# Four small reorderings at the end of a two-layer cross-attention kernel

What is changed: the second MLP weights of the next-to-last batch are built on GpSimd, the delays before three norms of the last batch and after the first turned rows are longer, and in the last layer two kinds of tiles get a second buffer.

## The chip, the cores and the metric

The kernel runs on one core of a Trainium2 chip. The time is the device time of one execution in microseconds (us). The core has five engines, each with its own instruction queue worked off in order: TensorE (PE, matrix products), VectorE (DVE), ScalarE (ACT), GpSimd (POOL) and SyncE (SP, which here only starts DMAs). A transfer that a kernel calls indirect takes its row numbers from a tile and is issued on POOL.

## The reference, cut to what matters

Everything is float32. `x` and the context are 16 batches of 256 rows of 256 numbers. There are two layers, each an attention and an MLP with a residual, with a layer norm before each.

```python
x = x + _L0_xattn_ref(ctx, _layernorm(x), ...)   # 8 heads of 128; keys: context and latents (512)
x = x + _L0_ffn_ref(_layernorm(x), ...)          # 256 -> 1024 -> 256
x = x + _L1_xattn_ref(_layernorm(x), ctx, ctx, ...)
x = x + _L1_ffn_ref(_layernorm(x), ...)          # 8 experts, 256 -> 256 -> 256, gated
```

In the first MLP the weights depend on the batch: products of rows of its own input are added to them.

```python
m1 = (even[:, :4, :, None] * odd[:, :4, None, :]).reshape(Bx, Hx, Dx)
m2 = (even[:, 4:, :, None] * odd[:, 4:, None, :]).reshape(Bx, Dx, Hx)
h = jnp.einsum('bsd,hd->bsh', x, W1) + scale * jnp.einsum('bsd,bhd->bsh', x, m1) + b1
h = jax.nn.gelu(h, approximate=False)
out = jnp.einsum('bsh,oh->bso', h, W2) + scale * jnp.einsum('bsh,boh->bso', h, m2) + b2
```

In the last layer each row has a weight for each of 8 experts, from a sigmoid; weights outside a zone are zero, so a row needs only some of the experts. The output of a row is the weighted sum of its experts, added to the row.

## The kernel before, in words

**Layer 0, attention.** A loop over `n`, the 128 pairs of batch and head, is the backbone. For each pair it computes queries (`s0q`) and keys (`s0k`), scores and softmax (`s1`, scaled on POOL in `s1_scale`, L902), turns the probabilities through DRAM (`s2` transposes blocks of 32 on DVE and sends them, L910 to L914; `s2_fetch` brings them back, L923), and multiplies with the values (`s3`, the product `po`).

**The chain of a batch.** What follows for a batch, output projection (`px`), norm, first MLP (`ph`, gelu, `pf`), norm, second attention (`pv1`, `pq1`, `sc1`, `po1`), norm and routing logits (`pl`), is a Python generator, `chain` (L332). It starts two heads into the next batch. For batches up to 13 (`hopped`) tensors are turned through DRAM; for batches 14 and 15 PE turns them with an identity matrix (`turned_tile`). Each norm sums on DVE, takes the root on POOL (`ln_rstd`, L261 and L262) and is applied on DVE (`ln_apply`, L267). `plus_row` (L312) adds a bias row on POOL.

In the first MLP `w2_block` (L432) multiplies, for each of 4 blocks and 2 halves, rows of the batch with its columns (L435), and `w2_add` adds the fixed weights on DVE (L443). `pf` needs these `W2e` and the gelu's `hT`, which ACT computes after loading a table.

**Routing.** `route` (L628) computes the expert weights of a batch, numbers its rows within each expert (`pn`), and scatters each row into its slot with 16 indirect DMAs per batch on POOL (L718, two at a time between other work).

**The last layer.** `experts` (L1229) runs over groups of up to 4 tiles of 128 rows of one expert. Batches 0 to 9 are the first part (experts 0 to 7, three groups each), batches 10 to 15 the second. A group's rows are loaded from their slots (L1137), turned (the first two groups by PE, `turn_rows`; the others through DRAM, `send_rows` and `fetch_rows`), and go through `gate` (`pg`), `up` (`pu`) and `down` (`pd`). `down` scales the result on DVE into a tile `o` (L1219) and adds it to the output rows in DRAM with an indirect DMA on POOL (L1220), 128 in all. Scatters of one expert have distinct rows and do not wait for each other; the first one of the next expert of the same part waits until those of the expert before have landed.

**What sets the order.** All of it is issued by one program, so each engine's order is the order in which Python calls are made. `Clock.pe` counts the PE time issued so far. A generator yields the PE time to wait before it goes on; `gap` (L114) runs, between the pieces of the backbone and after it, the first job in `line` whose time has come. So the numbers in `yield` decide where a step stands in every engine's queue. The generators of the change are those of batches 13 to 15 and of the experts, which run side by side from the last heads of batch 15 on.

**Pools.** `D_.wk` (L1110) is opened after the last head's scores, `D_.more` (L1113) when the last projection has been issued. A tile asked of a pool with all its buffers in use makes its writer wait.

Of the kernel before, what the change touches and what calls it, by code (L numbers as in the profile page):

```python
# [12 lines left out]
F32 = mybir.dt.float32  # L13
# [6 lines left out]
P = 128  # L20
# [9 lines left out]
def xattn_ffn_kernel(  # L30
# [10 lines left out]
    nc = tc.nc  # L41
    B, S, D = x.shape
# [21 lines left out]
    wk = ctx.enter_context(tc.tile_pool(name="work_c", bufs=1))  # L64
# [3 lines left out]
    def mm_tile(n, name):  # L68
        return psum.tile([P, n], F32, tag="mm", bufs=6, name=name, padded_shape=[P, 512])
# [9 lines left out]
    def mm(out, lhsT, rhs, **kw):  # L79
        nc.tensor.matmul(out, lhsT, rhs, **kw)  # L80
        Clock.pe += max(0.38, 1.667e-3 * math.prod(out.shape[1:]))
# [23 lines left out]
    def apart(ins, group, others=()):  # L105

        for g in (group, *others):
            tc.declare_no_dep(
                ins.ins, group=g, reason="rows of one group go to different places"
            )  # L110
        tc.add_to_no_dep_group(group, ins.ins)
        nc.gpsimd.nop()
# [65 lines left out]
    for k, n in enumerate(NTOKS):  # L178
        t = sum(NTOKS[:k]) // P
# [78 lines left out]
    def ln_rstd(mv, tag):  # L258

        rs = small.tile([P, TC], F32, tag=f"rs{tag}", bufs=2, name=f"rs_{tag}")  # L260
        nc.gpsimd.tensor_scalar(rs, mv[:, :, 1], EPS, None, ALU.add)  # L261
        nc.gpsimd.tensor_tensor(rs, rs, mhalf, ALU.pow)  # L262
        return rs
# [21 lines left out]
    def to_blocks(pool, src, C, tag, bufs, name, most=None):  # L285
        tb = pool.tile(
            [P, C * D], F32, tag=tag, bufs=bufs, name=name, padded_shape=[P, most or C * D]
        )
        tb = tb.rearrange("p (m d c s) -> p m d c s", m=QP, d=DC, c=C)
        for c in range(C):  # L290
            nc.vector.transpose(
                tb.rearrange("p m d c s -> p d m c s")[:, :, :, c, :],
                src[:, c, 0:D].rearrange("p (d m r) -> p d m r", d=DC, m=QP),
            )
        hop = dram.tile([P, QP, DC * C * QB], F32, tag=f"{tag}{C}", name=f"hop_{name}")
        nc.sync.dma_start(hop, tb.rearrange("p m d c s -> p m (d c s)"))
        return hop
# [34 lines left out]
    def chain(b, A, behind):  # L332
# [11 lines left out]

        hopped = b < B - 2

        def raw_tile(tag, name):
            return wk.tile([P, QP, DC, TC, QB], F32, tag=tag, name=name)

# [20 lines left out]


        rs = ln_rstd(mv, "b")
        yield 2.5


        while behind is not None and b - 1 not in A.fed:
# [55 lines left out]
        def w2_block(c):  # L432
            for d in range(DC):

                (nc.gpsimd if hopped else nc.vector).tensor_tensor(  # L435
                    W2e[:, c, d, :].rearrange("p (i a) -> p i a", i=NI),
                    evs[1][:, :, c * NA : (c + 1) * NA],
                    od[:, d, NI : 2 * NI].unsqueeze(2).to_broadcast([P, NI, NA]),
                    ALU.mult,
                )  # L440
# [40 lines left out]
        for c in range(NI):  # L481
            w2_block(c)
            yield 1.7
            w2_add(c)
# [17 lines left out]


        rs = ln_rstd(mv, "q")
        yield 2.5
        while behind is not None and not behind.done:
            yield 0.4
        y = wk.tile([P, TC, D], F32, tag="y", name=f"yc_{b}")
# [7 lines left out]
        sent = Clock.pe + SENT  # L516
# [72 lines left out]

        rs = ln_rstd(mv, "d")  # L590
        nc.sync.dma_start(out[b].rearrange("(c p) d -> p c d", p=P), x_b)

        yield 2.8 if b < B - 1 else 6.0
        while b >= 2 and not A.tails[b - 2].done:
            yield 0.4
        row = A.row[b] = wk.tile([P, TC, ROW], F32, tag="row", bufs=2, name=f"row_{b}")
# [141 lines left out]
    with ExitStack() as sh, ExitStack() as sa, ExitStack() as sf:  # L738
# [352 lines left out]
        def add_chain(b, behind):  # L1091
            job = Job(chain(b, A, behind))
            A.tails[b] = Job(route(b, A, job))
            line.extend([job, A.tails[b]])
            return job


        TG = 4
        NG = TG * P

        class D_:


            w, wk, more = {}, None, None


        def open_front():
# [8 lines left out]
        def load_expert(e):  # L1116
            k = len(D_.w)
            pool = D_.front if k == 0 else D_.wk if k == 1 else D_.more
            w = D_.w[e] = pool.tile([P, 3, DC, D], F32, bufs=1, name=f"wx_{e}")
            nc.sync.dma_start(w[:, 0], Wg[e].rearrange("(c p) i -> p c i", p=P))  # L1120
            nc.sync.dma_start(w[:, 1], Wu[e].rearrange("(c p) i -> p c i", p=P))
            nc.sync.dma_start(w[:, 2], Wd[e].rearrange("(c p) d -> p c d", p=P))

        class G:
# [44 lines left out]
                )  # L1169

            def send_rows(self):
                self.hop = to_blocks(D_.wk, self.rows, self.tiles, "tbd", 1, f"rows_{self.name}_b", TG * D)

            def fetch_rows(self):
                self.take()
# [32 lines left out]
            def down(self, t):  # L1208
                if t >= self.tiles:
                    return  # L1210
                w = D_.w[self.e]
                pd = mm_tile(D, f"pd_{self.name}_{t}")
                for i in range(IC):
                    mm(
                        pd, self.hT[:, i, ts(t, P)], w[:, 2, i, :],
                        start=(i == 0), stop=(i == IC - 1),
                    )
                o = D_.wk.tile([P, D], F32, tag="o", bufs=9, name=f"o_{self.name}_{t}")
                nc.vector.tensor_scalar(o, pd, self.wt[:, t : t + 1], None, ALU.mult)  # L1219
                ins = nc.gpsimd.indirect_dma_start(  # L1220
                    out=out_rows[0 : sum(NTOKS[: self.part + 1]), :],
                    out_offset=bass.IndirectOffsetOnAxis(ap=self.at[:, t : t + 1], axis=0),
                    in_=o, in_offset=None, compute_op=ALU.add,
                )
                apart(
                    ins, f"out_{self.part}_{self.e}", [f"out_{1 - self.part}_{e}" for e in range(E)]
                )

        def experts(groups, ready=None):  # L1229

            if groups[0].e not in D_.w:
                load_expert(groups[0].e)
            for g in groups[:2]:
                g.load()
            yield 7.0
            while D_.wk is None:
                yield 0.4
            for d in range(DC):
                groups[0].turn_rows(d)
                yield 2.0  # L1240
            late = None
            for n, g in enumerate(groups):
                if n == 0:
                    groups[2].load()
                if n + 3 < len(groups):
                    while ready is not None and not ready(groups[n + 3]):
                        yield 0.4
                for i in range(IC):
                    g.gate(i)
                    yield  # L1250
                    g.up(i)
                    yield
                    if n == 0:
                        groups[1].turn_rows(i)
                    if n + 2 < len(groups):
                        if i == 0:
                            groups[n + 2].send_rows()
                        else:
                            groups[n + 2].fetch_rows()
                    if i == 0 and n + 3 < len(groups):  # L1260
                        groups[n + 3].load()
                    if late is not None:
                        late.down(2 * i)
                        late.down(2 * i + 1)
                        yield
                ahead = groups[min(n + 3, len(groups) - 1)].e
                if ahead not in D_.w and (len(D_.w) < 2 or D_.more is not None):
                    load_expert(ahead)
                if n + 2 < len(groups) and groups[n + 2].e not in D_.w:
                    while D_.more is None:  # L1270
                        yield 0.4
                    load_expert(groups[n + 2].e)
                late = g
            for t in range(late.tiles):
                late.down(t)
# [21 lines left out]
        for n in range(NS + 2):  # L1297
            b, h = divmod(n, H)
            if h == 2 and b > 0:
                last = add_chain(b - 1, last)  # L1300
            more = bulk(b, h) if n < NS else None
            if n < NS:
                s1(n)
            if n == NS - 4:
                sf.close()
                open_front()
                rest = Job(experts(
                    lists,
                    lambda g: g.part == 0 or B - 1 in A.tails and A.tails[B - 1].done,
                ))  # L1310
                line.append(rest)
# [48 lines left out]
        with tc.If(some > 0):  # L1360
            drain(experts(groups(0, "+", (4, 3, 3)) + groups(1, "+", (3, 3))))
# [38 lines left out]
```

## Time and profile before

| | |
|---|---|
| median of 3 runs | 1845.97 us (1845.02 to 1847.69) |
| profiled execution | 1845.63 us |
| its span, first to last instruction | 1843.6 us |
| mean granted TensorE clock | 0.994 |
| matmul time on PE | 1808.7 us |
| POOL: scatters to the output, L1220 | 128 of 1.57 us |
| POOL: scatters to the slots, L718 | 256 of 0.99 us |
| last matmul starts at | 1828.05 us |
| last scatter starts at | 1832.96 us |

Times in the profile count from the span's start. A row of the timeline has start, duration, engine, line, operation, output and inputs, and in brackets the idle time before it with what the profile takes for its end. The duration of an indirect DMA on POOL is that of its issue; its data land later. An idle time's releaser is the semaphore event that came last, which need not be the one that was waited for.

### The profile page before, as it was taken

The page shows a single profiled execution, that of the slowest core. Times are in us where ns is not written, and L with a number is a line of the kernel's source. Part 1 is how long each engine was busy: PE and PEld are TensorE (multiplying, and loading weights), DVE is VectorE, ACT ScalarE, POOL GpSimd, SP SyncE. Part 2 cuts the span into 40 slices and gives each one's busy share as a digit, 9 for nine tenths or more (in the row PEclk, how much of TensorE's full clock was granted, in tenths as well). Part 3 has the DMA queues.
Part 4 walks back from the last instruction along what each step waited for, and adds up shares of the span by engine and source line. Part 5 has one row for each costly group of instructions (what it writes and reads, how often), then busy time and mean ns, then how long its engine had stood idle before and what let it go on. Part 6 is the DMA issues. An engine that isn't in the chain of part 4 may idle for free.

```text
span 1843.6 us, 22696 instructions
## 1 busy us (share of the span) xinstructions
PE 1808.7 (98%) x6600; PEld 1230.4 (67%) x6600; DVE 1212.0 (66%) x3349; ACT 583.2 (32%) x1298; POOL 846.4 (46%) x980
## 2 busy tenths in 40 slices
PE   8999999999999999999999999999999999999996
PEld 4666666666666666666667676767676676666664
DVE  5456585858585858586767676757566676655553
ACT  3443333333434333333333333333333321111110
POOL 2123235353535353535353535353524178766655
PEclk9999999999999999999999999999999999999998
DMA  6553546464646465645455556464636478999986
GB/s 223 180 183 121 165 148 203 153 201 153 205 146 205 161 197 161 195 156 198 161 193 164 190 164 197 154 204 146 202 103 222 133 215 193 238 242 225 214 204 100
DMA packets 271181, 332.72 MB, mean 180 GB/s; under 512 B 31388, under 2 KB 222792, under 8 KB 271048
## 3 DMA queue, kind: packets, MB, share of 16 engines
q1 hardware_dynamic: 240280, 279.63, 48.2%
q0 software_dynamic: 30720, 51.54, 12.2%
q8 instruction: 55, 0.90, 0.2%
q14 instruction: 78, 0.64, 0.1%
q10 hardware_dynamic: 48, 0.01, 0.0%
HBM read 165.77 MB, written 165.28 MB: 180 GB/s over the span
## 4 chain that ended last, share of the span: by engine, by line
PE 93%; DVE 3%; DMA 1%; issue 1%; POOL 1%; SPq 0%; ACT 0%; ACTq 0%; DVEq 0%; POOLq 0%
PE po L80 13%; PE pv L80 13%; PE sc L80 13%; PE pk L80 11%; PE pq L80 7%; PE px L80 6%; PE ph L80 6%; PE pg L80 6%; PE pf L80 6%; PE pu L80 5%; PE pd L80 5%; PE pl L80 1%; POOL out_dram L1220 0%; DVE tb L910 0%; PE pn L80 0%
## 5 line engine op out<-in xcount | busy, mean ns | idle before, releaser
L902 POOL TENSOR_SCALAR pr<-pr,ri 128x512 f32<-128x512 f32 x256 | 179.4, 711 | 319.5 <-DVE ri L901 314.5
L894 ACT ACTIVATE pr<-sc,nm 128x512 f32<-128x512 f32 x256 | 173.5, 682 | 478.3 <-DVE nm L888 405.9
L718 POOL DMA_INDIRECT slots_d<-row,at_slot x256 | 253.3, 989 | 70.4 <-issue 70.4
L1220 POOL DMA_INDIRECT out_dram<-o,at x128 | 201.2, 1572 | 100.6 <-issue 26.5
L80 PE MATMUL po<-pT,v 128*128 128x256 f32 x1024 | 242.1, 379 | 1.3 <-DVE W2T L955 0.7
L80 PE MATMUL sc<-kT,qT 128*128 128x512 f32 x512 | 241.1, 593 | 1.5 <-ACT kT L827 1.5
L80 PE MATMUL pk<-kvT,Wk_sb 128*128 128x512 f32 x512 | 240.6, 592 | 0.0
L80 PEld LDWEIGHTS po<-pT,v 128*128 128x128 f32 x1024 | 194.4, 190 | 69.2 <-issue 37.5
L80 PE MATMUL pv<-Wv_sb,kvT 128*128 128x512 f32 x512 | 235.2, 592 | 0.0
L940 DVE TENSOR_SCALAR outT<-po,cvec 128x256 f32<-128x256 f32 x128 | 61.0, 477 | 250.6 <-PE po L80 229.6
L910 DVE STREAM_TRANSPOSE tb<-pr 128x512 f32<-128x512 f32 x256 | 165.8, 685 | 6.9 <-DMA hop<-tb 6.5
L80 PEld LDWEIGHTS pv<-Wv_sb,kvT 128*128 128x128 f32 x512 | 97.1, 190 | 107.3 <-issue 102.1
L888 DVE TENSOR_REDUCE nm<-sc 128x1 f32<-128x512 f32 x256 | 160.2, 662 | 2.0 <-PE sc L80 1.9
L80 PEld LDWEIGHTS sc<-kT,qT 128*128 128x128 f32 x512 | 96.9, 190 | 70.1 <-issue 61.2
L80 PEld LDWEIGHTS pk<-kvT,Wk_sb 128*128 128x128 f32 x512 | 97.3, 190 | 67.8 <-issue 61.2
L80 PE MATMUL pg<-yTd,wx 128*128 128x384 f32 (+3 forms) x328 | 127.1, 510 | 7.9 <-DVE yTd L829 5.7
L80 PE MATMUL pq<-kvT,Wq_sb 128*128 128x256 f32 x512 | 132.8, 382 | 0.0
L1195 ACT ACTIVATE sg<-pg 128x384 f32<-128x384 f32 (+3 forms) x82 | 41.3, 503 | 278.3 <-PE pg L80 244.7
L80 PEld LDWEIGHTS pq<-kvT,Wq_sb 128*128 128x128 f32 x512 | 96.4, 191 | 42.1 <-issue 28.5
L80 PE MATMUL pd<-wx,hTd 128*128 128x256 f32 x512 | 123.9, 379 | 0.6 <-DVE hTd L1206 0.6
L80 PE MATMUL pu<-yTd,wx 128*128 128x384 f32 (+3 forms) x328 | 123.7, 500 | 0.0
L825 ACT COPY v<-pv 128x512 f32<-128x512 f32 (+1 forms) x132 | 70.6, 535 | 164.9 <-PE pv L80 163.9
(205 smaller groups left out, 2700.3 us busy)
## 6 DMA issues: line engine op xcount, KB each, us to landing
hop<-tb SPq DMA_DIRECT2D x128, 512.0 KB
pT<-hop SPq DMA_DIRECT2D x512, 128.0 KB
ev<-ev_d SPq DMA_DIRECT2D x32, 512.0 KB
rows<-slots_d SPq DMA_DIRECT2D x31, 397.5 KB
hop_rows_b<-rows_b SPq DMA_DIRECT2D x30, 384.0 KB
yTd<-hop_rows_b SPq DMA_DIRECT2D x120, 96.0 KB
rows<-slots_d SPq DMA_DIRECT2D x8, 530.0 KB
cin<-in_ctx_dram SPq DMA_DIRECT2D x16, 256.0 KB
```

The lines of the kernel that those rows point to most:

```text
L80: nc.tensor.matmul(out, lhsT, rhs, **kw)
L718: ins = nc.gpsimd.indirect_dma_start(out=slots_d[part], out_offset=bass.IndirectOffsetOnAxis(ap=at_slot[:, c, e : e + 1], axis=0), in_=row ...
L825: nc.scalar.copy(out, src)
L888: nc.vector.tensor_reduce(nm, sc, AX.X, ALU.max, negate=True)
L894: nc.scalar.activation(pr, sc, AF.Exp, bias=nm, accum_out=sm)
L902: nc.gpsimd.tensor_scalar(pr, pr, ri, 1.0, ALU.mult, ALU.mult)
L910: nc.vector.transpose(tb[:, :, c, :], heads[n][c][0].rearrange("p (m f) -> p m f", m=QP))
L940: nc.vector.tensor_scalar(o, po, col("bv", h), None, ALU.add)
L1195: nc.scalar.activation(self.sg, self.pg, AF.Tanh, scale=0.5)
L1220: ins = nc.gpsimd.indirect_dma_start(out=out_rows[0 : sum(NTOKS[: self.part + 1]), :], out_offset=bass.IndirectOffsetOnAxis(ap=self.at[:, ...
```

## The change

1. `w2_block` runs on GpSimd for batch 14 too; only batch 15 keeps it on VectorE.
2. A batch's three delays after a norm's sums are named `queued`: unchanged for batches up to 14 (2.5, 2.5, 2.8), and 6.7, 6.7 and 7.0 for batch 15 (before: 2.5, 2.5, 6.0).
3. After each of the first group's two turns the experts wait 4.0 instead of 2.0.
4. The blocks `tbd` of `send_rows` (one buffer) and the tiles `o` of `down` (nine) are taken in turn from `D_.wk` and, once it is open, `D_.more`, so that there are two and eighteen.

```diff
+        queued = 2.8 if b < B - 1 else 7.0
...
         rs = ln_rstd(mv, "b")
-        yield 2.5
+        yield queued - 0.3
...
-                (nc.gpsimd if hopped else nc.vector).tensor_tensor(
+                (nc.gpsimd if b < B - 1 else nc.vector).tensor_tensor(
...
         rs = ln_rstd(mv, "q")
-        yield 2.5
+        yield queued - 0.3
...
         nc.sync.dma_start(out[b].rearrange("(c p) d -> p c d", p=P), x_b)
-
-        yield 2.8 if b < B - 1 else 6.0
+        yield queued
...
-            w, wk, more = {}, None, None
+            w, wk, more, sent, made = {}, None, None, 0, 0
...
             def send_rows(self):
-                self.hop = to_blocks(D_.wk, self.rows, self.tiles, "tbd", 1, f"rows_{self.name}_b", TG * D)
+
+                D_.sent += 1
+                pool = D_.more if D_.sent % 2 and D_.more is not None else D_.wk
+                self.hop = to_blocks(
+                    pool, self.rows, self.tiles, "tbd", 1, f"rows_{self.name}_b", TG * D
+                )
...
-                o = D_.wk.tile([P, D], F32, tag="o", bufs=9, name=f"o_{self.name}_{t}")
+                D_.made += 1
+                pool = D_.more if D_.made % 2 and D_.more is not None else D_.wk
+                o = pool.tile([P, D], F32, tag="o", bufs=9, name=f"o_{self.name}_{t}")
...
             for d in range(DC):
                 groups[0].turn_rows(d)
-                yield 2.0
+                yield 4.0
```

## The prediction

> **What bounds the kernel now.** I read the page first. It shows TensorE (PE) busy all the way, with GpSimd (POOL) full only in the last stretch.
>
> ```profile
> PE 1808.7 (98%) x6600; PEld 1230.4 (67%) x6600; DVE 1212.0 (66%) x3349; ACT 583.2 (32%) x1298; POOL 846.4 (46%) x980
> PE   8999999999999999999999999999999999999996
> POOL 2123235353535353535353535353524178766655
> PE 93%; DVE 3%; DMA 1%; issue 1%; POOL 1%; SPq 0%; ACT 0%; ACTq 0%; DVEq 0%; POOLq 0%
> ```
>
> The change acts only from about 1420 us on (the last heads of batch 15, and the expert layer). So I asked next what PE waited for after 1395.
>
> ```profile
> PE pg L80 <- DVE yTd L829: 5.7, 1, 5.7
> PE ycT_p L84 <- DVE yc L267: 2.5, 1, 2.5
> PE pg L80 <- DVE o L1219: 1.9, 1, 1.9
> ```
>
> These three holes are what an eye on PE would go for. Third, the timeline of POOL from 1476 to the end, which carries the forecast:
>
> ```profile
> 1478.15 1.10 POOL L718 DMA_INDIRECT slots_d<-row,at_slot  x1 [0.19 <-issue]
> 1479.56 0.97 POOL L718 DMA_INDIRECT slots_d<-row,at_slot  x1 [0.30 <-issue]
> ...
> 1514.51 1.60 POOL L1220 DMA_INDIRECT out_dram<-o,at  x1 [0.30 <-issue]
> 1519.31 1.57 POOL L1220 DMA_INDIRECT out_dram<-o,at  x1 [3.20 <-DMA out_dram<-o,at]
> ...
> 1580.37 1.56 POOL L1220 DMA_INDIRECT out_dram<-o,at  x1 [0.30 <-issue]
> 1587.68 1.55 POOL L1220 DMA_INDIRECT out_dram<-o,at  x1 [5.75 <-DVE sg L1205]
> ...
> 1660.56 1.58 POOL L1220 DMA_INDIRECT out_dram<-o,at  x1 [0.30 <-DMA out_dram<-o,at]
> ...
> 1829.22 1.58 POOL L1220 DMA_INDIRECT out_dram<-o,at  x1 [0.30 <-issue]
> 1831.10 1.55 POOL L1220 DMA_INDIRECT out_dram<-o,at  x1 [0.31 <-DMA out_dram<-o,at]
> 1832.96 1.56 POOL L1220 DMA_INDIRECT out_dram<-o,at  x1 [0.30 <-issue]
> ```
>
> And two rows of VectorE (DVE), the tiles that the scatters of 1660.56 and 1832.96 add into the output:
>
> ```profile
> 1639.24 0.48 DVE L1219 TENSOR_SCALAR o<-pd,wt 128x256 f32<-128x256 f32 x1 [0.38 <-issue]
> 1828.79 0.48 DVE L1219 TENSOR_SCALAR o<-pd,wt 128x256 f32<-128x256 f32 x1 [0.80 <-PE pd L80]
> ```
>
> So POOL is 20.8 us behind at 1660 and still 3.7 us behind at the end. From 1478.15 it stops only where a new expert's first scatter has to wait until the scatters of the expert before have landed (1514.51 to 1519.31, 1580.37 to 1587.68; the releaser named there, an early DVE step, had long been done). The page's chain runs through PE because PE hardly idles; the order of this stage is POOL's. A scatter starts every 1.87 us, a routing scatter (L718) every 1.28, a norm's pair takes 1.25, a row addition (L312) 1.45. With these, 1478.15 plus 16 routing scatters (20.5), a norm (1.25), an addition (1.45) and seven scatters (13.1) gives 1514.45; the row says 1514.51. The queue is full.
>
> **The change, part by part.** The profiled execution took 1845.63 us (span 1843.6, so 2.0 around it), 0.34 under the median of 1845.97; the sum is made against 1845.63. What is moved I take from the instruction order of the two programs.
>
> *Second weights of batch 14 on GpSimd.* Eight blocks (L435) leave DVE (8 x 0.41 = 3.3 us) for POOL (8 x 0.61 = 4.9; median of the 112 such rows of earlier batches). On POOL two stand before the scaling of head 6 (L902), six between that and head 7. POOL is idle there (8.35 us before 1432.75), the rows they read were issued at 1412.19, and head 6's scaling still starts at 1423.0: 0 on the path. The GpSimd rows range only from 0.61 to 1.06 us beside a busy DVE, so I add nothing for interference. The Trainium skill (SBUF — State Buffer, Who interferes with whom) says that a VectorE instruction with two SBUF inputs and a GpSimd instruction that reads SBUF lock each other out; by it the three weight additions on DVE beside the six blocks could each wait 0.61, and the sum below would be 1.8 us longer.
>
> *Turned rows at 4.0 instead of 2.0.* The first gate now stands behind the last MLP's output product (pf, 16 of its 32 passes, then head 5's po, then the rest). PE's first hole does not close, it changes owner: pf needs the gelu. On DVE the blocks' time is partly taken by the norm of batch 13's rows, which now stands ahead of them; the score maxima of head 7 end at about 1429.5 instead of 1430.6. The same ACT rows follow (two exponentials, table load 1.28, gelu 1.91; before, the gelu ended at 1434.74), so pf starts at about 1433.7, against 1432.64 for the gate before. Half clock till 1436.58 as before: PE is 0.5 later.
>
> A second, new wait: the next group's second turned tile is copied by ACT only behind the two exponentials of batch 14's attention. From the end of the scores that took 1.8 us before (1463.5 to 1465.3), plus 0.5 for the copy; the gate there has 0.3 + 0.65 of work to cover it. 1.5 us of hole; between 0 (if ACT gets there first) and 2.4 (the whole of it).
>
> *Where the POOL queue starts.* The first two scatters of expert 0 ran at 1463.20 and 1465.17 in idle time. Now their products come behind the last projection (px) and batch 14's turn, 41.7 us of PE work after pf's start, plus 0.5 and 1.5 as above: about 1476.9. DVE then has the projection's statistics (1.3), the slot numbers (1.2) and four row transposes (1.42) ahead of the tile (0.44): POOL gets it at about 1479.0. Against the old start of 1478.15 that is +0.85; two more scatters in the full queue, +3.74; one norm that now lies before it, -1.25. **+3.4**. Bounds: 1475.4 if nothing on DVE stands before the tile and there is no second hole (-0.2), 1481 with half clock after it (+5.4).
>
> *Which routing scatters lie in a landing wait.* The total of them is the same, the places are not. Before, one pair of batch 14 (1550.82, 1552.10) ran between the last scatter of expert 1 and the first of expert 2, and one of batch 15 in the wait from 1609.63 to 1618.26 (expert 3 to 4). Both cost nothing there. Now each stands behind the wait, among scatters: 2 x 2.56 = **+5.1** (0 to 5.1, 0 if the wait shortens because less is queued ahead). The first wait was 5.62, with tile and landing arriving together; the nearest one without a pair is 4.80 to 5.4: **-0.5**.
>
> *What else is moved past.* On SP the load of the third group's rows goes behind head 7's blocks, from 1435.8 to about 1448; its transposes come at about 1455, and the next such load (issued 1455.77, transposed 1461.12 without a wait) took at most 5.4: hidden. The first load of the second part's rows waits on SP for the last routing scatter, which moves from 1657.4 to about 1669; SP may stand from about 1665 to 1675, with the blocks of two later groups behind it. PE has two groups (some 17 us) in hand by then, so 0; if that cover were gone, PE would stand up to 10 us, of which POOL's backlog swallows all.
>
> *Delays of 6.7, 6.7, 7.0 for batch 15.* They place other PE work before the turn of yc: the second hole (2.46, and half clock 1538.98 to 1542.39, that is 4.2 together) mostly closes. The clock rows are clear: a 3.41 us window with 0.03 us of matmul is followed by one at 0.50. The Trainium skill (TensorE: Matmul & The Clock Gate, Why this matters for your kernels) warns only of gaps over about 3 us; by it this hole would be worth 2.5. Either way it shortens PE alone, worth 0 to 4.2 there and 0 at the end while POOL is behind.
>
> *Two buffers of blocks and 18 output tiles.* They take away the 1.9 us wait for an output tile and waits of the row blocks (0.3 to 0.5 on PE). POOL's scatters use tiles that are ready long before: 0. With cover gone (POOL caught up) all this is worth PE's sum: +0.5 +1.5 -4.2 -0.3 -2.0 -0.5 = -5.0.
>
> Sum: +3.4 +5.1 -0.5 = **+8.0**, so 1853.6 us, 0.4% slower than the median. Of it the thirteen landing waits (4.80 to 8.62, mean 6.3) are taken as they were.
>
> **The rivals.**
> *POOL's queue starts early, or one pair is still hidden.* For it: the lower bounds above. Start at 1475.4 and one pair lost: -0.2 +2.6 -0.5 = +1.9, 1847.5: no difference that a measurement of this kernel tells (0.2%, 3.7 us). Against it: DVE's order before the tile is written in the program.
> *PE is the bound, and all its closed holes count.* POOL must then lose its backlog. One mechanism can do it: PE, with 18 tiles and two block buffers, runs further ahead, its block traffic leaves the DMA queues sooner, and scatters land faster. It decides from a mean landing wait of 5.4 (13 x 0.9 = 11.7 undoes +8.0 and gives -3.7); at the shortest, 4.80, PE limits: -5.0 and the 3.4 us that the last tile waits now, 1837.2. For it: waits without traffic are the short ones. Against it: the traffic's amount is the same, DMA is at 0.9 to 1.0 from 1580 to 1800, and POOL's own pace of 1.87 is untouched.
> *More is lost.* The new hole halves the clock (+1.7), the first one grows by the interference, and the landing waits at the expert changes rise by half a microsecond each because pairs are queued right before them (+6.5): 1858 to 1861.
>
> **How the numbers follow.** Main case (+4 to +12) 0.63; no difference 0.16; PE-bound and faster 0.11; more lost 0.10. Slower by over 0.2%: 0.73. The likeliest is 1853.6, its own range 1849.7 to 1857.6. For 8 in 10 the range takes in the no-difference case and most of the last: 1845 to 1859.5.
>
> **What would show it.** Right: the last scatter on POOL at about 1841 while PE's last matmul ends near 1824; pf waiting for the gelu about 6.7 us near 1427; no long wait of the turn of yc; first output scatter near 1479, and no L718 between the last scatter of expert 1 and the first of expert 2. Wrong: a last scatter within 1 us of the last tile (PE is the bound), landing waits with a mean under 5.4, or the first output scatters before 1476.

## The result, and the profile after

The changed kernel takes 1855.14 us (median of 6 runs, 1854.20 to 1857.64) against 1845.49 us (6 runs of the kernel before): ratio 1.0053, 95% interval 1.0040 to 1.0066. It is slower by 0.5%. The profiled execution took 1854.39 us; its span is 1852.7 us, 9.1 more than before.

The busy times and the 40 slices on the page of the changed kernel, for PE and POOL:

```profile
PE 1810.5 (98%) x6600; PEld 1234.7 (67%) x6600; DVE 1208.8 (65%) x3341; ACT 582.6 (31%) x1298; POOL 852.1 (46%) x988
...
PE   8999999999999999999999999999998999999995
...
POOL 2123235353535353535353535353525177766666
```

PE's matmul time rose by 1.8 us only. An eye on PE would not find nine microseconds here. What PE waited for after 1395 (in total, times, longest), all waits of 0.2 us and more:

```profile
PE pf L80 <- ACT hT L475: 7.1, 1, 7.1
PE pf L80 <- DVE W2e L445: 3.2, 2, 1.9
PE pg L80 <- ACT yTd L826: 0.9, 1, 0.9
PE pd L80 <- DVE hTd L1212: 0.2, 1, 0.2
```

The first hole changed its owner, from the turned rows to the gelu; the waits for `yc` and for an output tile are gone; a wait for the second weights of batch 15 is new, and the prediction did not have it. Third, POOL's timeline (start, duration, instruction, idle time before it), with line numbers eight higher than before for the output scatters (L1228) and one for the routing scatters (L719):

```profile
1480.92 1.68 POOL L1228 DMA_INDIRECT out_dram<-o,at  x1 [2.02 <-DVE o L1227]
...
1545.33 1.59 POOL L1228 DMA_INDIRECT out_dram<-o,at  x1 [0.70 <-DVE o L1227]
...
1555.40 1.60 POOL L1228 DMA_INDIRECT out_dram<-o,at  x1 [0.30 <-issue]
1560.41 1.56 POOL L1228 DMA_INDIRECT out_dram<-o,at  x1 [3.41 <-DVE o L1227]
...
1618.72 1.61 POOL L1228 DMA_INDIRECT out_dram<-o,at  x1 [0.30 <-DVE o L1227]
1624.29 1.56 POOL L1228 DMA_INDIRECT out_dram<-o,at  x1 [3.96 <-DVE o L1227]
...
1841.92 1.56 POOL L1228 DMA_INDIRECT out_dram<-o,at  x1 [0.30 <-issue]
```

The last tile that a scatter adds, on DVE:

```profile
1831.18 0.48 DVE L1227 TENSOR_SCALAR o<-pd,wt 128x256 f32<-128x256 f32 x1 [0.79 <-PE pd L80]
```

The last scatter starts 10.25 us after its tile is finished; before, it was 3.69. POOL sets the end, by more than before. Between the last scatter of expert 1 (1555.40) and the first of expert 2 (1560.41) no routing scatter lies any more, nor between 1618.72 and 1624.29.

**Where the time came from, stretch by stretch.** The execution after runs 0.61 us late already before the change acts (the last transposition of the first turned rows starts at 1427.30, before at 1426.69). So I count both from that transposition. Times to POOL's first scatter of each expert of the first part, of the second part, and to the last scatter; the forecast column adds up the terms of the prediction in the stretches where they fall:

| first scatter of | before | after | difference | forecast |
|---|---|---|---|---|
| expert 2 | 127.85 | 133.11 | +5.3 | +2.9 |
| expert 3 | 160.99 | 169.45 | +8.5 | +5.5 |
| expert 4 | 191.57 | 196.99 | +5.4 | +5.5 |
| expert 5 | 225.65 | 231.28 | +5.6 | +5.5 |
| expert 6 | 251.85 | 259.78 | +7.9 | +8.0 |
| expert 7 | 273.68 | 282.63 | +9.0 | +8.0 |
| second part | 286.71 | 295.68 | +9.0 | +8.0 |
| last scatter | 406.27 | 414.62 | +8.4 | +8.0 |

The end is met within half a microsecond, but two stretches on the way are off, by +2.4 (up to expert 2) and by -3.0 (expert 3 to 4). The experiments below ask whether POOL's queue is the cause at all, which part fills it, and what these two errors are. Times in them are compared by ratio with runs of the kernel before on the same chip; 0.1% is 1.85 us.

### The profile page after: what moved, and what is told of

Its sections match the earlier page's. It is cut to its first block, busy times and chain, and to the rows that moved or that the text cites. A ratio compares the mean times of both kernels' runs of the same rounds, so it can differ in the third digit from the quotient of the medians.

```text
span 1852.7 us, 22641 instructions
## 1 busy us (share of the span) xinstructions
PE 1810.5 (98%) x6600; PEld 1234.7 (67%) x6600; DVE 1208.8 (65%) x3341; ACT 582.6 (31%) x1298; POOL 852.1 (46%) x988
## 5 line engine op out<-in xcount | busy, mean ns | idle before, releaser
L719 POOL DMA_INDIRECT slots_d<-row,at_slot x256 | 253.2, 989 | 70.7 <-issue 69.8
L1228 POOL DMA_INDIRECT out_dram<-o,at x128 | 201.5, 1574 | 96.6 <-DVE o L1227 36.2
L80 PE MATMUL pf<-W2e,hT 128*128 128x256 f32 x512 | 123.6, 391 | 10.4 <-ACT hT L475 7.1
L80 PE MATMUL pq<-kvT,Wq_sb 128*128 128x256 f32 x512 | 133.0, 382 | 0.0
## 6 DMA issues: line engine op xcount, KB each, us to landing
rows<-slots_d SPq DMA_DIRECT2D x31, 397.5 KB
```

The lines of the kernel that those rows point to most:

```text
L719: ins = nc.gpsimd.indirect_dma_start(out=slots_d[part], out_offset=bass.IndirectOffsetOnAxis(ap=at_slot[:, c, e : e + 1], axis=0), in_=row ...
L1228: ins = nc.gpsimd.indirect_dma_start(out=out_rows[0 : sum(NTOKS[: self.part + 1]), :], out_offset=bass.IndirectOffsetOnAxis(ap=self.at[:, ...
```

## Experiments: one part at a time

**The turned rows alone.**

```diff
                 groups[0].turn_rows(d)
-                yield 2.0
+                yield 4.0
```

> The kernel before with the turned rows alone at 4.0. Theory (GpSimd's queue of indirect DMAs sets the end): +6.0 us. The first output scatter comes at about 1479 and takes two more scatters into the full queue (+3.4); in this program's order one pair of routing scatters still lies between the last scatter of expert 1 and the first of expert 2, the other pair has left the change from expert 3 to 4 (+2.6). Rival (TensorE sets the end): its two holes, +0.5 and +1.5, so +2.0 us. A third possibility, that the start alone counts and a pair behind the landing wait costs nothing: +3.4.

Measured: 1858.09 us against 1846.76, ratio 1.0064 (1.0051 to 1.0077), +11.8 us (9.4 to 14.2). This part alone costs the whole loss and more; all three numbers that I had for it were too small. PE's waits in this kernel, the three longest:

```profile
PE pf L80 <- ACT hT L473: 7.9, 1, 7.9
PE pf L80 <- DVE W2e L443: 3.7, 2, 3.0
PE pg L80 <- DVE W1e L427: 1.7, 1, 1.7
```

and POOL's timeline at expert 1:

```profile
1548.11 0.96 POOL L718 DMA_INDIRECT slots_d<-row,at_slot  x1 [0.30 <-issue]
1552.65 1.59 POOL L1220 DMA_INDIRECT out_dram<-o,at  x1 [3.59 <-DVE o L1219]
```

PE stands for the weights of batch 15, the tiles of expert 1 come late, and POOL, which was to be full from 1479 on, runs dry for 3.6 us at 1549. The first scatter of expert 2 comes 137.85 us after the turned rows, 10.0 later than before.

**The delays of batch 15 alone.**

```diff
+        queued = 2.8 if b < B - 1 else 7.0
...
         rs = ln_rstd(mv, "b")
-        yield 2.5
+        yield queued - 0.3
...
         rs = ln_rstd(mv, "q")
-        yield 2.5
+        yield queued - 0.3
...
-        yield 2.8 if b < B - 1 else 6.0
+        yield queued
```

> The kernel before with the delays of batch 15 alone (6.7, 6.7, 7.0). Theory (GpSimd's queue): the queue starts where it did; a pair leaves the wait from expert 3 to 4 (+2.6), a row addition of 1.45 us enters the wait from expert 1 to 2 (-1.45): +1.1 us. Rival (TensorE sets the end): the hole before the turn of yc closes, -4.2 us.

Measured: 1848.01 us, ratio 1.0006 (0.9994 to 1.0017): +1.1 us, between -1.1 and +3.1. The rival's -4.2 is excluded. PE did gain: its last tile comes 397.5 us after the turned rows, before 402.1. POOL's last scatter comes at 408.0, before 406.3. A gain of 4.6 us on the engine that is busy 98% of the span did not reach the end.

**Two buffers alone.**

```diff
-            w, wk, more = {}, None, None
+            w, wk, more, sent, made = {}, None, None, 0, 0
...
-                self.hop = to_blocks(D_.wk, self.rows, self.tiles, "tbd", 1, f"rows_{self.name}_b", TG * D)
+                D_.sent += 1
+                pool = D_.more if D_.sent % 2 and D_.more is not None else D_.wk
+                self.hop = to_blocks(
+                    pool, self.rows, self.tiles, "tbd", 1, f"rows_{self.name}_b", TG * D
+                )
...
+                D_.made += 1
+                pool = D_.more if D_.made % 2 and D_.more is not None else D_.wk
-                o = D_.wk.tile([P, D], F32, tag="o", bufs=9, name=f"o_{self.name}_{t}")
+                o = pool.tile([P, D], F32, tag="o", bufs=9, name=f"o_{self.name}_{t}")
```

> The kernel before with the two block buffers and 18 output tiles alone; the order of GpSimd's instructions is the one of before. Theory (GpSimd's queue): 0.0 us, and TensorE's last product 2.4 us earlier. Rival (TensorE sets the end): -2.4 us.

Measured: 1846.28 us, ratio 1.0001 (0.9990 to 1.0011), +0.2 us between -1.8 and +2.0. The -2.4 of the rival lies outside. PE's last tile moved by 0.6 us only (401.5 after the turned rows), not by 2.4, so the second half of my expectation was too large as well.

**Second weights of batch 14 alone on GpSimd.**

```diff
-                (nc.gpsimd if hopped else nc.vector).tensor_tensor(
+                (nc.gpsimd if b < B - 1 else nc.vector).tensor_tensor(
```

> The kernel before with the second weights of batch 14 alone on GpSimd. Theory: 0.0 us, the eight rows lie in GpSimd's idle time before the queue fills. Rival (the two engines hold each other up at SBUF): +1.8 us. GpSimd rows of 0.61 speak for the first, rows of 1.06 for the second.

Measured: 1845.39 us, ratio 0.9992 (0.9983 to 1.0001), -1.5 us between -3.1 and +0.2. The rule on the shared lock (the Trainium skill, SBUF — State Buffer, Who interferes with whom) could have made it +1.8; the time does not show that. The trace shows rows of both engines slower side by side in one place: the weight addition of 1426.02 on DVE in the changed kernel took 1.07 us, the other three 0.66 to 0.70, and of the eight GpSimd rows the two from 1426.50 on took 1.06 us, the others 0.60 to 0.64. That is the rule's kind of overlap, worth 1.3 us in sum over the two engines, and it did not reach the end. In the profiled execution of this part alone PE's last tile even came 3.7 us earlier than before, its first hole being 4.3 us instead of 5.7.

**All but the turned rows.** The changed kernel with `yield 2.0` back:

> The changed kernel with the turned rows back at 2.0; the other three parts stay. Theory: GpSimd's queue starts as before, and the three parts alone gave +1.1, 0 and -1.5 within about 2 us each: between -1.5 and +1.5 us. Rival (TensorE sets the end): -6.6 us. If the parts add their harm to each other rather than through the queue's start: +3 or more.

Measured: 1844.50 us against 1846.96, ratio 0.9980 (0.9969 to 0.9991), -3.7 us between -5.7 and -1.7. Slightly better than I allowed, and not the rival's -6.6: PE's last tile comes 398.5 us after the turned rows (before 402.1), the last scatter 403.4 (before 406.3), 4.4 us behind its tile. So the other three parts are worth a little, and the turned rows alone turn the gain into a loss.

## Experiments: is it POOL's queue?

**Ten scatters less.** In both kernels the ten output scatters of expert 1 of the first part are left out (the output lacks their rows):

```diff
                 nc.vector.tensor_scalar(o, pd, self.wt[:, t : t + 1], None, ALU.mult)
+                if self.part == 0 and self.e == 1:
+                    return
                 ins = nc.gpsimd.indirect_dma_start(
```

The kernel before without them:

> The kernel before without the ten output scatters of expert 1 of the first part (the output tiles are still made; their rows are missing from the output). Theory (GpSimd's queue sets the end): the queue loses ten scatters (18.7 us) and one landing wait, far more than its backlog at the end (3.7 us), so TensorE's last product sets the end: -3.4 us. Rival (TensorE sets the end already): 0.

The changed kernel without them:

> The changed kernel without the same ten scatters (the same rows are missing). Theory: GpSimd is 10.25 us behind TensorE at the end of the changed kernel; with the backlog gone the end follows TensorE's last product, 10 us earlier: -0.4 us against the kernel before, and 2.4 to 3 above the kernel before without the same scatters, which is TensorE's own sum for the change (the prediction had -5.0 for it). Rival (the time is lost elsewhere than in GpSimd's queue): +9 as in the changed kernel.

Measured: 1839.63 us, ratio 0.9959 (0.9946 to 0.9972), -7.6 us, for the one; 1852.48 us, ratio 1.0022 (1.0009 to 1.0034), +4.1 us, for the other (its runs spread from 1847.4 to 1855.4, and the profiled one, 1854.8, is among the longest). Both expectations missed, the theory's and the rival's. In neither run does PE set the end: the last scatters still start 4.6 and 10.5 us after their tiles are finished. POOL, idle until expert 2, falls behind again from there; in the profiled execution of the changed kernel its last scatter comes 414.9 us after the turned rows, with the ten scatters 414.6. What the missing scatters did change is PE. Its waits after 1395 in the kernel before without the ten scatters:

```profile
PE pg L80 <- DVE yTd L829: 5.7, 1, 5.7
PE pf L80 <- DVE W2e L443: 0.3, 1, 0.3
PE pd L80 <- DVE hTd L1206: 0.2, 1, 0.2
```

The wait for `yc` (2.5 us before) and the one for an output tile (1.9) are gone without any change to delays or buffers. They were POOL's doing: the norm of `yc` takes its root on POOL, and in the kernel before that root stood behind scatters. Its timeline in the kernel before:

```profile
1533.27 1.60 POOL L1220 DMA_INDIRECT out_dram<-o,at  x1 [0.30 <-issue]
1535.18 0.97 POOL L718 DMA_INDIRECT slots_d<-row,at_slot  x1 [0.30 <-issue]
1536.45 0.96 POOL L718 DMA_INDIRECT slots_d<-row,at_slot  x1 [0.30 <-issue]
1537.43 0.26 POOL L261 TENSOR_SCALAR rs_q<-mv_q 128x2 f32<-128x2 f32 x1
```

With POOL idle there (its root at 1533.17), PE's last tile comes 394.8 us after the turned rows, 7.3 earlier than in the kernel before. In the changed kernel PE's waits stay as they were without the ten scatters (7.1, 3.2, 0.9, 0.2), and its last tile comes at 403.9 with or without them. So PE's own price of the change, with the queue out of its way, is +9.1 us. It adds up: the first hole 7.1 instead of 5.7 (+1.5), half clock behind it 2.8 instead of 2.0 (+0.8), the new gate 0.9, the weights of batch 15 3.2 instead of 0.3 (+2.9) and the half clock behind them 3.0.

**What holds the first scatter of expert 2?** From that scatter to the last one POOL needs 275.1 to 283.8 us in all kernels with unchanged group order here (278.4 before, 281.5 after), so of the 8.4 us that the last scatter loses 5.3 lie ahead of that scatter. Two things could hold it: PE's wait for the weights, or the full queue. The two kernels without the ten scatters show PE's side alone, because POOL is idle there until the tile comes (first the kernel before, then the changed one):

```profile
1550.54 1.61 POOL L1222 DMA_INDIRECT out_dram<-o,at  x1 [7.22 <-DVE o L1219]
1560.93 1.61 POOL L1230 DMA_INDIRECT out_dram<-o,at  x1 [7.28 <-DVE o L1227]
```

That is 123.3 and 132.6 us after the turned rows. In the kernel before, the same scatter comes at 127.85, 4.5 us later, held up by the queue and by the hole that the queue makes in PE's work; in the changed kernel PE alone holds it until half a microsecond before its 133.11. DVE in the changed kernel, from the first of these waits on, has no free time (start, duration, instruction):

```profile
1523.58 0.68 DVE L445 TENSOR_TENSOR W2e<-W2e,W2T 128x512 f32<-128x512 f32 x1
1524.18 0.75 DVE L437 TENSOR_TENSOR W2e<-ev,od 128x256 f32<-128x256 f32 x2
1524.85 1.09 DVE L291 STREAM_TRANSPOSE rows_b<-rows 128x256 f32<-128x256 f32 x3
1525.87 0.84 DVE L1227 TENSOR_SCALAR o<-pd,wt 128x256 f32<-128x256 f32 x2
1526.62 0.69 DVE L445 TENSOR_TENSOR W2e<-W2e,W2T 128x512 f32<-128x512 f32 x1
...
1529.03 0.72 DVE L445 TENSOR_TENSOR W2e<-W2e,W2T 128x512 f32<-128x512 f32 x1
```

The last addition (1529.03) was at 1526.04 in the kernel before, where PE waited 0.3 us for it. I took away the four additions (the weights of batch 15 then lack their common part):

```diff
         def w2_add(c):
+            if b == B - 1:
+                return
```

> The changed kernel without the four additions to the second weights of batch 15 on VectorE (its weights lack their common part, so the rows of batch 15 come out different). Theory (GpSimd's queue sets the end): TensorE's two waits for these weights and the half clock behind them, 6.6 us together, go, and its last product comes that much earlier, but GpSimd waited for tiles there by only 0.3 us twice: -0.6 us against the changed kernel, +9 against the kernel before. Rival (TensorE's lost time is what the change costs): -6.6 against the changed kernel, +3 against the kernel before.

then the first two output scatters (their rows are missing):

```diff
+                if self.part == 0 and self.first + t * P < 2 * P:
+                    return
                 ins = nc.gpsimd.indirect_dma_start(
```

> The changed kernel without its first two output scatters (the first two tiles of expert 0; their rows are missing). Theory: they stand at the head of a queue that never runs empty again, so the end comes two scatters earlier, -3.7 us against the changed kernel, +6 against the kernel before. Rival (the queue waits for tiles later, so that its start does not count): 0 against the changed kernel, +9.6 against the kernel before.

and, those two having been measured, both together:

> The changed kernel without the four additions of batch 15 and without its first two output scatters, both at once (rows of batch 15 and of two tiles come out different). In the two runs before, each alone left the first scatter of expert 2 where it was in the changed kernel (within 0.3 us, measured from the last turned row). Theory (two chains tie there, GpSimd's full queue and TensorE's stall for these weights): only both together move it, by the 3.7 us of the two scatters less what the landing wait from expert 0 to 1 takes back (1.7 in the run without the two): 2 to 3.7 us earlier, and the end by as much, so +1.5 to +4 against the kernel before. Rival (the place is held by something else, such as the landing waits or the tiles' own time): it stays, and the time is that of the run without the additions, +5.

Measured, with the first scatter of expert 2 counted from the turned rows:

| kernel | first scatter of expert 2 | last scatter | ratio to the kernel before |
|---|---|---|---|
| before | 127.85 | 406.3 | 1 |
| changed | 133.1 | 414.6 | 1.0053 (1.0040 to 1.0066) |
| without the additions | 133.0 | 413.0 | 1.0029 (1.0017 to 1.0041) |
| without the two scatters | 132.7 | 415.2 | 1.0039 (1.0026 to 1.0052) |
| without both | 131.1 | 410.7 | 1.0023 (1.0013 to 1.0034) |

Each alone leaves the scatter within half a microsecond of where it was, both move it by 2.0 us. POOL's rows there, without the additions:

```profile
1555.28 1.60 POOL L1230 DMA_INDIRECT out_dram<-o,at  x1 [0.31 <-issue]
1561.16 1.56 POOL L1230 DMA_INDIRECT out_dram<-o,at  x1 [4.28 <-DVE ri L584]
```

without the two scatters:

```profile
1555.55 1.60 POOL L1230 DMA_INDIRECT out_dram<-o,at  x1 [0.30 <-issue]
1560.37 1.57 POOL L1230 DMA_INDIRECT out_dram<-o,at  x1 [3.22 <-DVE o L1227]
```

and without both (the last turned row of the three runs starts at 1428.18, 1427.63 and 1428.50):

```profile
1553.69 1.60 POOL L1232 DMA_INDIRECT out_dram<-o,at  x1 [0.30 <-issue]
1559.60 1.57 POOL L1232 DMA_INDIRECT out_dram<-o,at  x1 [4.31 <-DVE x L588]
```

So two chains nearly tie here, within about half a microsecond: the queue that starts late (the prediction's term) and PE's stall for weights (not in the prediction). The tile's end says the same: it lay 0.85 us ahead of this scatter in the changed kernel, 0.70 without the two scatters, where PE's stall remains, and 6.7 without the additions, where only the queue can hold it. But each place is that of one profiled execution, and the landing wait right ahead of the scatter was 5.01 us in the changed kernel, 5.88, 4.82 and 5.91 in these three; the last scatter ahead of that wait had moved by 1.0, 0.2 and 2.9 us.

By the time it is less clear. The run without the additions is 4.4 us faster than the changed kernel by the ratios, where I had expected 0.6 and the trace shows 1.6 at the last scatter (the profiled execution, 1853.75, was the longest of its six); its interval and that of the changed kernel leave anything between about 1 and 8. PE's last tile came only 2.2 us earlier there than in the changed kernel, and not 6.6, because with the stall gone PE met another wait, for a norm of batch 15:

```profile
PE ydT_p L84 <- DVE row L267: 2.8, 1, 2.8
```

The sums of that norm were ready at 1562.02, but its root starts on POOL only at 1570.41, behind scatters: again a hole that the queue makes. The run without the two scatters is 2.6 us faster than the changed kernel by the ratios, between the theory's 3.7 and the rival's 0, and the intervals exclude neither. The run without both came 4.2 us over the kernel before (2.4 to 6.3), just above the theory's +1.5 to +4 and not apart from the rival's +5. Where the whole of that time lies stays open.

## Experiment: take the landing waits out of the queue

If landing waits in POOL's queue keep PE's gains from the end, an order in which other rows' scatters stand behind a change of expert should free them. On the changed kernel with the turned rows back at 2.0, the groups of the second part come between those of the first from expert 6 on, so that four changes of expert are covered; the routing scatters must then be done earlier:

```diff
+        sixth = 3 * (E - 2)
+        second = lists[len(first) - 1 :]
+        lists = (
+            lists[: sixth + 2] + second[0:2]
+            + [first[sixth + 2]] + second[2:4]
+            + [first[sixth + 3]] + second[4:6]
+            + [first[sixth + 4]] + second[6:]
+        )
...
-                    yield 2.6 if b < B - 2 else 5.2
+                    yield 2.6
```

> The same without the turned rows, with two more edits: the groups of the second part of the tokens come between those of the first from expert 6 on, so that four changes of expert have scatters to other rows behind them, and the routing scatters are spread at 2.6 instead of 5.2. Theory (the landing waits in GpSimd's queue are what keeps TensorE's gains from the end): four waits of 4.3 us leave the queue, 17 us, more than its backlog, and TensorE sets the end, 4.2 + 2.4 earlier than before and without the 3.4 us of backlog: -10 us, or -6 if the second part's first rows arrive a little late. Rival (the landing waits are not the reason, or the rows of the second part come too late): 0 or above.

Measured: 1846.19 us, ratio 0.9992 (0.9981 to 1.0003): no gain. POOL was only 1.2 us behind PE at the end, as the theory has it, but PE waited 4.5 us for `yc`: with batch 14's routing scatters at 2.6 more of them stand in front of the root of that norm. The same hole as above, made by the same queue. So the routing scatters of batch 14 went back:

```diff
-                    yield 2.6
+                    yield 5.2 if b == B - 2 else 2.6
```

> The interleaved order again, with the routing scatters of batch 14 back at 5.2 and only those of batch 15 at 2.6, so that the norm before the turn of yc isn't held up in GpSimd's queue. Theory: that wait (4.5 us and the half clock behind it, 6 to 7 us) goes, GpSimd follows TensorE to the end, which comes near 1824 in the trace: -5 to -6 us against the kernel before, -3 to -4 against the order without interleaving. Rival (something else holds TensorE, or the landing waits grow when scatters of both parts share the queue): the same as the first interleaved kernel, -0.8.

Measured: 1840.06 us against 1847.42, ratio 0.9964 (0.9951 to 0.9977), -6.6 us between -9.1 and -4.2, 0.9% below the changed kernel by the two ratios. The last tile, on DVE:

```profile
1825.34 0.48 DVE L1227 TENSOR_SCALAR o<-pd,wt 128x256 f32<-128x256 f32 x1 [0.79 <-PE pd L80]
```

and POOL in the interleaved part and at its end:

```profile
1726.24 1.54 POOL L1228 DMA_INDIRECT out_dram<-o,at  x1 [1.49 <-DVE o L1227]
...
1733.99 1.54 POOL L1228 DMA_INDIRECT out_dram<-o,at  x1 [2.48 <-DVE o L1227]
...
1827.05 1.54 POOL L1228 DMA_INDIRECT out_dram<-o,at  x1 [0.30 <-issue]
```

Where POOL waits in the interleaved part, it waits for PE's tiles, and its last scatter starts 1.2 us after the last tile. This version beats both kernels. Not all of the 6.6 us comes from the new order: the same kernel without it and without the earlier routing scatters of batch 15 was already 3.7 us under the kernel before (ratio 0.9980). The two ratios leave 3.0 us for these two edits, and their intervals anything from 6 us to nothing; the traces show the lag of the last scatter behind its tile going from 4.4 to 1.2 us.

## Why the prediction was right, and where it was not

It said 1853.6 us, slower, because POOL's queue of indirect transfers sets the end; it is 1855.14. That the queue sets the end is shown: the last scatter at 1841.92 (forecast about 1841) follows its tile by 10.25 us, a gain of 4.6 us on PE from the delays does not reach the end, and in the interleaved order the lag shrinks to 1.2 us. That the size came so near is partly luck: two errors of opposite sign, +2.4 us up to expert 2 and -3.0 from expert 3 to 4, cancel, and PE's stall for weights, which the forecast did not have, hardly shows only because the late queue alone would have cost nearly the same there. Step by step:

- *Second weights of batch 14 on GpSimd: 0.* Right within 3.1 us below and 0.2 above.
- *Turned rows, first hole: the wait for the gelu.* Right in kind (7.1 us, forecast about 6.7), too small in size: +0.5 was forecast, +2.3 measured. The product behind it started 0.4 us later than forecast, and above all the half clock did not end at 1436.58 but went on to 1440.28.
- *The new wait at the gate of the second group: 1.5.* It was 0.9, with ScalarE as releaser, as forecast.
- *Where POOL's queue starts: +3.4.* The first output scatter came at 1480.3 on the clock of before (1480.92 less 0.61), not 1479.0, because the first hole cost 1.8 us more than forecast and the new gate 0.6 less; with two scatters more (3.7) and one norm less (1.2) that is +4.7. The step that failed is the one left out beside it: the later steps of batches 14 and 15 collide on DVE, the second weights of batch 15 come late, PE stands 3.2 us, and up to expert 2 the loss is +5.3 instead of +2.9. The full queue alone would have given nearly the same, as the tie shows. In the kernel with the turned rows alone the stall is longer, POOL runs dry, and the loss is 11.8.
- *Two pairs of routing scatters no longer hidden: +5.1.* Right for the first pair: the stretch that it moved into grew by 3.2 (forecast 2.6; 0.6 of it is a longer landing wait). Wrong for the second: the wait from expert 3 to 4 had been taken as unchanged without the pair, but shrank from 8.62 to 5.57. So the term was worth -0.7 in this trace (-3.0 there, +2.3 where the pair stands now) and +1.0 by the means given below, not +2.6. The lower end of the bound named this ("0 if the wait shortens because less is queued ahead"); I chose the upper.
- *Wait from expert 1 to 2: -0.5.* It fell from 5.62 to 5.01.
- *Transfers on SP hidden: 0.* PE's list of waits has none for a transfer after the change. Right.
- *Delays of batch 15, two buffers: 0 at the end.* Right within the intervals of each part alone, which exclude the rivals' -4.2 and -2.4. One row was misread there: the window with 0.03 us of matmul is 2.48 us long, not 3.41; the 3.41 us ahead of the half clock (1535.57 to 1538.98) held 0.96 us of matmul.
- *PE's own sum, -5.0, and its end near 1824.* Wrong, and the worst step: PE's last tile came at 1831.18, +1.8 against the turned rows. The holes named did close, but the stall for weights was missing (2.9 us more of wait and 3.0 of half clock behind it), and the first hole cost 1.8 more. With the queue out of its way PE's price is even +9.1, because the closed holes (`yc`, the output tile) were the queue's own doing in the kernel before: 7.3 us were gone there as soon as POOL was idle. The PE-bound rival would not have given 1837 but a slower kernel too.
- *Landing waits taken as they were.* Thirteen of 4.80 to 8.62 with mean 6.3 became thirteen of 5.01 to 7.92 with mean 6.15. In sum right; from one run to the next single ones differ by one or two microseconds.

## What to carry to other kernels

An engine at 98% need not set the end: compare, for the last piece of work, when its input was ready and when it started, and ask whether the engine's holes are not made by the other queue. A delay that moves a step moves everything its generator issues later; look for the place where two batches' steps now meet on another engine, here DVE, as closely as for the step itself. And work that seems hidden in another transfer's landing wait may be prolonging that wait: its price is known only when the same wait is seen without it.

## What the runs showed of the hardware

*Short gaps halved the clock, and for two windows.* The changed kernel in stretches of 3.4 us around the stall for weights (columns after the stretch: its length, busy time and instructions of PE, of weight loads, DVE, ScalarE and POOL, granted clock, DMA share, GB/s):

```profile
1525.40:1528.80 3.40, 1.18 (x5) 0.68 (x4) 3.30 (x13) 0.00 (x0) 3.02 (x2) 1.00 0.61 139
1528.80:1532.20 3.40, 2.39 (x6) 1.95 (x7) 1.13 (x4) 0.00 (x0) 2.87 (x2) 0.53 1.07 209
1532.20:1535.60 3.40, 3.40 (x10) 2.69 (x9) 0.82 (x3) 0.00 (x0) 2.79 (x3) 0.50 0.63 67
1535.60:1539.00 3.40, 3.40 (x15) 2.61 (x14) 1.47 (x4) 0.00 (x0) 2.76 (x4) 0.96 0.60 97
```

PE's two gaps of 1.91 and 1.32 us, with 1.18 us of matmul in the window of the first, were followed by a granted clock of 0.53, and the next window, which follows one with 2.39 us of matmul, still had 0.50. The Trainium skill (TensorE: Matmul & The Clock Gate, Why this matters for your kernels) warns of gaps over about 3 us; here less was enough, and the measurement decides. But the length of a gap alone does not tell: the gap of 2.46 us before `yc` in the kernel before was followed by 3.41 us at half clock, the one of 2.76 us in the run without the additions by none, and so was the one of 1.88 us for an output tile in the kernel before.

*A landing wait was shorter when no routing scatters stood in it, but whether they prolong it is not shown.* The wait from expert 3 to 4, from scatter to scatter, was 8.62, 7.29, 8.23 and 7.22 us with a pair inside (the kernel before, buffers alone, weights alone, the kernel before without the ten scatters; mean 7.84), and 5.57, 6.10, 7.59, 5.84, 6.38, 6.04, 6.59 and 6.22 without (the changed kernel, turned rows alone, delays alone, all but the turned rows, the changed kernel without the ten scatters, and the last three of the table above; mean 6.29). In the two interleaved kernels, with a pair inside, it was 9.18 and 7.07. By the two means about 1.0 of the pair's 2.56 us was hidden. Two things change at once, though: where the pair is not in the wait, it stands right ahead of the last scatter of expert 3, which gives the scatters before it longer to land. And the wait from expert 2 to 3, with no pair inside in any kernel, was 5.68 to 8.53 us with mean 7.40, so a wait of that length needs no pair. What in the transfer takes this time no run here shows.
